# A fused conv, Mamba and MLP kernel: selective scan by quads of groups instead of pairs, depthwise sums on TensorE, and a job list by earliest end

## The chip, the cores and the metric

The kernel runs on one core of one Trainium2 chip. The metric is device time in microseconds (us) of that core, from the start to the end of one execution. All data is fp32. The engines work side by side, each through its own queue in order: PE (TensorE, matrix multiplication), DVE (VectorE), ACT (ScalarE), POOL (GpSimd) and SP, which here issues every DMA transfer.

## The reference

The input x has 8 images of 384 channels and 32 x 32 pixels. Four layers follow each other, each behind a group normalisation (32 groups of 12 channels) and with the input added to the output. Layer 0 is a Mamba block over the 1024 pixels of an image, layer 1 a patch-wise Fourier filter between two 1x1 convolutions with a depthwise 3x3 convolution and a gate, layer 2 a LayerNorm, another Mamba block and an MLP, layer 3 a depthwise 3x3 convolution. What matters here:

```python
# Mamba, layers 0 and 2: D_INNER 768, D_STATE 16, L 1024 steps, B 8 images
dt = softplus(dt @ dt_proj_w.T + dt_proj_b)
A = -exp(A_log)
def step(h, inp):
    dt_t, B_t, C_t, u_t = inp
    dA = exp(dt_t[..., None] * A)
    h = dA * h + (dt_t * u_t)[..., None] * B_t[:, None, :]
    y = einsum('bdn,bn->bd', h, C_t)
    return (h, y)
y = ys + u * D
y = y * silu(z)
out = y @ out_proj_w.T
# layer 1, in its middle; layer 3 is the same kind of convolution alone
t = conv_general_dilated(t, w_dw, padding='SAME', feature_group_count=hid)   # 3x3
g = gelu(x1) * x2
# layer 2, after its Mamba block
t = gelu(t @ mlp_w1.T + mlp_b1) @ mlp_w2.T + mlp_b2
```

## The kernel before, in words

**Chunks, pairs and quads.** The work is cut into chunks of 512 steps: 8 images x 2 halves x 2 Mamba layers = 32 chunks, 16 of layer 0 and then 16 of layer 2. A chunk has 768 channels x 16 states = 12288 recurrences, which lie 128 to a tile: 96 groups of 8 channels x 16 states, each a scan of [128, 512]. Two groups make a *pair*; 48 pairs make a chunk (PAIRS, L41). Four groups, two neighbouring pairs, make what the change calls a *quad*; there are 24 in a chunk, 768 in all.

**The steps of a pair.** `begin` (L512) issues the transfer of g, [128, 2, 512], 512 KB, from a DRAM scratch (dud) that repeats dt*u over the 16 states. `times` (L521) multiplies g by B on POOL. `decay` (L529) makes two matmuls with 32 rows each, which repeat dt over the states into two of four PSUM banks dA0 to dA3, and two exps on ACT, in place. `scan` (L540) runs two tensor_tensor_scan on DVE. On even pairs (`pool_pair`, L508, with some exceptions in EXTRA, L50) the scan writes to PSUM, in place, and DVE multiplies the result by C, from PSUM into g (L558), and copies the last column to `carry`. On the others the scan writes to g in SBUF, ACT copies the carry and POOL multiplies by C (`after_scan`, L560, the instruction at L566). `gather` (L570) sums over the states with four matmuls per two pairs into y, each into another 32 rows of PSUM; after four such sums comes the product with D, and `gate` (L588) multiplies y by silu(z) on DVE. Neighbouring pairs take turns with the two halves of the four banks, so one pair can be decayed while the other is scanned.

**The other work** is written as Python generators that are advanced between the pairs ("jobs"): `measure` (group statistics of an image), `front` (normalise, project, taps of the short convolution, dt and the spill of dt*u to DRAM), `gates` (project and silu of z), `finish` (out_proj, and in layer 2 the `mlp`), `layer1` and `layer3`. `step_dt` (L461) makes a matmul and softplus for one of six blocks of dt, then dt*u on POOL (`times_u`, tile du, L478) and four transfers to DRAM (`spill`, tile dud, L485). `mlp` (L773) streams its weights from DRAM: `load_up` (L780, tile mw1, 192 KB, four buffers) two blocks ahead of their matmuls ps_up, and `load_down` (L784, tile mw2, 384 KB, three buffers) two ahead of ps_dn. Three PSUM banks (NBANK) serve all jobs; `pipe` (L129) lets up to two units of a job fly, one stage to a call. The depthwise sums of layers 1 and 3 are eight or nine scalar_tensor_tensor on DVE per [96 or 128, 512] block (L731, L859), in PSUM.

**The order.** It is written out by hand (L906 to L945). For each pair t, in program order: begin(t+4), after_scan(t-1), times(t+2), decay(t+1), scan(t), possibly gate, then the jobs, and every second pair gather. Jobs stand in three lanes (fronts, ends, tails; L70); a lane advances its first job so that the count of pieces done follows a straight line between the job's first and last pair, from a table of expected pieces (PIECES, L66). SP's queue holds the transfers in the same program order.

Of the kernel before, what the change touches and what calls it, by code (L numbers as in the profile page):

```python
# [16 lines left out]
P = 128  # L17
# [5 lines left out]
NS = 16  # L23
# [14 lines left out]

E8 = 8
NSUB = 4  # L40
PAIRS = [(k, s, jp) for k in range(ND) for s in range(NSUB) for jp in range(2)]  # L41
NPAIR = len(PAIRS)
PER_K = NPAIR // ND
NH = ND // 2
NEAR = [(k, m) for k in range(KC) for m in range(KC) if abs(k - m) <= 1]
AHEAD = 4
NG = 8
NDT = 7
NBANK = 3
EXTRA = {"l0_": ((14,), (14,)), "l2_": ((), (6, 14))}  # L50
# [7 lines left out]
def _img(ap):  # L58
# [5 lines left out]
WAIT = "wait"  # L64

PIECES = {"gates": 8, "front0": 40, "front1": 45, "measure": 20, "end0": 5, "end1": 40,  # L66
          "layer1": 90, "layer3": 60}


class Lane:  # L70
# [3 lines left out]
    def __init__(self):  # L74
        self.jobs = deque()

    def add(self, kind, gen, first, last):
        self.jobs.append([kind, gen, first, last, 0])

    def step(self, t=None):  # L80

        for _ in range(4):
            if not self.jobs:
                return
            job = self.jobs[0]
            kind, gen, first, last, done = job
            if t is not None and done < PIECES[kind]:
                if done >= PIECES[kind] * (t + 1 - first) / (last - first):
                    return
            got = next(gen, self)  # L90
            if got is self:
                PIECES[kind] = done
                self.jobs.popleft()
            elif got is WAIT:
                return WAIT
            else:
                job[4] += 1
            if t is None:
                return
# [3 lines left out]
def tile_conv_preact_d4(ctx: ExitStack, tc: tile.TileContext, a: dict, out: bass.AP):  # L103
# [10 lines left out]
    live = {"ps": 0, "dt": 0}  # L114

    def mm(out_, lhsT, rhs, start=True, stop=True):
        nc.tensor.matmul(out_, lhsT, rhs, start=start, stop=stop)  # L117
# [11 lines left out]
    def pipe(units, deep=2):  # L129
# [4 lines left out]
        while units or flying:  # L134
# [7 lines left out]
            if units and live["ps"] < NBANK and len(flying) < deep:  # L142
# [9 lines left out]
            if units or flying:  # L152
                yield None if went else WAIT

# [27 lines left out]

    def rsqrt(out_, in_, eps):
        act(out_, in_, AF.Ln, bias=eps)
        act(out_, out_, AF.Exp, scale=-0.5)
# [13 lines left out]
    carry = const.tile([P, 2 * NPAIR], F32, name="carry")  # L199
# [9 lines left out]
    dAs = [psa.tile([P, T], F32, name=f"dA{q}") for q in range(4)]  # L209
# [3 lines left out]
    def group_stats(block):  # L213
# [3 lines left out]
        for h in range(2):  # L217
            for k in range(KC):
                v, then = block(h, k)
                nc.vector.bn_stats(st[:, k, h, :], v)  # L220
                then()
                yield
        for k in range(KC):
            nc.vector.bn_aggr(mv[:, k, :], _flat(st[:, k]))
        yield

        def group_mean(v):
# [11 lines left out]
            yield  # L239
# [6 lines left out]
        yield  # L246
# [4 lines left out]
        yield  # L251
# [4 lines left out]
        yield  # L256
        nbias = wk.tile([P, KC, 1], F32, tag="gnb", name="gnb", bufs=3)
        nc.gpsimd.tensor_mul(nbias, nmean, rstd)
        yield
# [9 lines left out]
    def load_mamba(pre):  # L269
# [4 lines left out]
        w["A"] = wk.tile([P, 2 * NPAIR], F32, tag="w_A", name="w_A", bufs=2)  # L274
# [12 lines left out]
        nc.vector.tensor_scalar_mul(w["A"], w["A"], -1.0)  # L287
# [6 lines left out]
    def load_out(w, pre):  # L294
        w["out"] = wk.tile([P, ND, C], F32, tag="w_out", name="w_out")
        load_rows(w["out"], a[pre + "out_proj"], ND)

# [6 lines left out]
    def measure(s):  # L304
# [11 lines left out]

        load(0)
# [6 lines left out]
        s["stats"] = yield from group_stats(block)  # L324
# [16 lines left out]
    def gates(s):  # L341

        z = s["z"] = [wk.tile([P, NH, T], F32, tag="z", name="z", bufs=2) for _ in range(2)]

        def evict(d):
            return lambda ps: act(z[d // NH][:, d % NH, :], ps, AF.Copy)

        yield from pipe(("ps_z", [both(project(s, d, DI), evict(d))]) for d in range(ND))
        yield
        for h in range(2):  # L350
            act(_flat(z[h]), _flat(z[h]), AF.Silu)
        s["gates"] = True
        yield

    def layer_norm(xn):
# [3 lines left out]
        yield  # L359
        for k in range(KC):  # L360
            nc.vector.tensor_sub(xn[:, k, :], xn[:, k, :], ps)
        ps_done()
        yield
# [5 lines left out]
        yield  # L369
        rsqrt(ps, ps, eps_ln)  # L370
        yield
        for k in range(KC):
            nc.vector.scalar_tensor_tensor(
                xn[:, k, :], xn[:, k, :], ln_w[:, k : k + 1], ps, ALU.mult, ALU.mult
            )
            if k == 0:
                yield
        ps_done()
        for k in range(KC):
            act(xn[:, k, :], xn[:, k, :], AF.Identity, bias=ln_b[:, k : k + 1])  # L380
        yield

    def front(s):

        c, n = s["c"], s["n"]
        xn = s["xn"] = load_half(s)
# [4 lines left out]
        yield  # L391
        yield
        for k in range(KC):
            group_norm(xn[:, k, :], xn[:, k, :], k, chunks[n - c]["stats"])
        yield
        if s["pre"] == "l2_":
            yield from layer_norm(xn)
        while n > 1 and "free" not in chunks[n - 2]:
# [14 lines left out]
        def taps(d):  # L413
            def run(ps):
                for j in (1, 2):
                    nc.vector.scalar_tensor_tensor(  # L416
# [7 lines left out]
            ("ps_in", [both(project(s, d, 0), tap(d)), taps(d)]) for d in range(ND)  # L424
# [14 lines left out]
        yield  # L439
        for h in range(2):  # L440
            act(_flat(uh[h]), _flat(uh[h]), AF.Silu)
        yield
        ps = yield from ps_tile("ps_x")
        for d in range(ND):
            mm(ps[:RX, :], w["x"][:, d, :], u[d], start=d == 0, stop=d == ND - 1)
            if d == NH - 1:
                yield
# [3 lines left out]
        yield  # L451
        bc = s["bc"] = wk.tile([P, 2, T], F32, tag="bc", name="bc", bufs=2)
        s["dt"], s["dud"] = [None] * ND, [None] * ND
# [7 lines left out]
        def step_dt(d):  # L461
# [10 lines left out]
            def plus(ps):  # L472
                v = s["dt"][d] = wk.tile([P, T], F32, tag="dt", name="dt", bufs=NDT)
                nc.vector.scalar_tensor_tensor(v, ps, 0.0, got["m"], ALU.max, ALU.add)
# [5 lines left out]
            def spill(ps):  # L480
                to = s["dud"][d] = dram.tile(
                    [2, NSUB * E8, 2, T], F32, tag="dud", name="dud", bufs=2 * ND
                )
                for j in range(4):
                    nc.sync.dma_start(  # L485
                        to[j // 2, :, j % 2, :], got["du"][32 * j : 32 * (j + 1), :]
                    )

            return [log, plus, None, times_u, spill]
# [4 lines left out]
        for d in range(ND):  # L494
            while live["dt"] >= NDT:
# [5 lines left out]
            yield  # L501
# [581 lines left out]
```

## Time and profile before

| | us |
|---|---|
| median of 3 runs | 8042.84 |
| lowest and highest | 8034.11, 8051.01 |
| the profiled execution's own time | 8035.86 |
| its span in the profile | 8034.1 |
| first scan starts | 90.5 |
| last gate of layer 0 starts | 3991.2 |
| last gate of layer 2 starts | 7884.7 |

The profiled execution was one of its own, beside the three runs. On the page, the first part gives each engine's busy time, its share of the span and the number of instructions; the second shows the span in 40 slices, with busy shares in tenths (9 is 90% or more) and under PEclk the TensorE clock that was granted. The groups give line, engine, operation, out<-in, shape and count, then busy time and mean duration (ns), then the idle time before them and what ended it. L117 and L181 are the helpers that record every matmul and every activation, so those are told apart by tile names. Each fp32 matmul is recorded as two passes. In a timeline, the columns are start, duration, engine, line, operation and count of merged instructions.

### The profile page before, as it was taken

The page shows a single profiled execution, that of the slowest core. Times are in us where ns is not written, and L with a number is a line of the kernel's source. Part 1 is how long each engine was busy: PE and PEld are TensorE (multiplying, and loading weights), DVE is VectorE, ACT ScalarE, POOL GpSimd, SP SyncE. Part 2 cuts the span into 40 slices and gives each one's busy share as a digit, 9 for nine tenths or more (in the row PEclk, how much of TensorE's full clock was granted, in tenths as well). Part 3 has the DMA queues.
Part 4 walks back from the last instruction along what each step waited for, and adds up shares of the span by engine and source line. Part 5 has one row for each costly group of instructions (what it writes and reads, how often), then busy time and mean ns, then how long its engine had stood idle before and what let it go on. Part 6 is the DMA issues. An engine that isn't in the chain of part 4 may idle for free.

```text
span 8034.1 us, 75941 instructions
## 1 busy us (share of the span) xinstructions
PE 7175.9 (89%) x23938; PEld 2930.4 (36%) x23938; DVE 5955.8 (74%) x7526; ACT 3747.6 (47%) x6393; POOL 5843.0 (73%) x2806
## 2 busy tenths in 40 slices
PE   6988898988989898998799999998999989899996
PEld 2223232322323232332343444344443444444444
DVE  4777879787887878788666686776867768677684
ACT  3445454444545444354444454444545545445542
POOL 5887877778878777777467676776767767677681
PEclk7878787887878788787798899898998989989988
DMA  5554555555455545555356565555565555655563
GB/s 136 142 140 119 132 132 125 130 131 138 126 138 129 131 122 128 136 139 136 79 142 157 137 168 153 139 161 149 158 162 146 149 152 153 167 139 160 145 173 90
DMA packets 403229, 1122.83 MB, mean 140 GB/s; under 512 B 52746, under 2 KB 106970, under 8 KB 402828
## 3 DMA queue, kind: packets, MB, share of 16 engines
q1 hardware_dynamic: 402828, 1117.98, 53.6%
q8 instruction: 192, 3.15, 0.2%
q14 instruction: 209, 1.71, 0.1%
HBM read 1042.28 MB, written 75.50 MB: 139 GB/s over the span
## 4 chain that ended last, share of the span: by engine, by line
PE 32%; DVE 8%; issue 6%; POOL 6%; ACT 3%; DMA 3%; SPq 1%; POOLq 0%; ACTq 0%; DVEq 0%
PE dA L117 7%; PE ps_dn L117 6%; POOL g L524 4%; PE y L117 4%; PE ps_up L117 4%; PE ps_z L117 3%; DVE g L545 2%; PE ps_out L117 2%; PE ps_in L117 2%; DVE dA L545 2%; POOL g L566 1%; DMA g<-dud 1%; PE ps_x L117 1%; DMA mw<-in_l_mlp_w 1%; ACT dA L181 1%
## 5 line engine op out<-in xcount | busy, mean ns | idle before, releaser
L524 POOL TENSOR_TENSOR g<-g,bc 128x1024 f32<-128x1024 f32 x1536 | 3588.7, 2353 | 14.5 <-ACT dA L181 11.3
L566 POOL TENSOR_TENSOR g<-g,bc 128x1024 f32<-128x1024 f32 x864 | 2031.6, 2351 | 1890.7 <-ACT carry L181 1109.5
L181 ACT ACTIVATE dA<-dA,w_A 128x512 f32<-128x512 f32 x3072 | 1911.5, 658 | 2708.6 <-PE dA L117 2558.4
L117 PE MATMUL dA<-dt,selr 32*128 32x512 f32 x6144 | 2224.3, 747 | 411.2 <-DVE g L558 320.0
L117 PEld LDWEIGHTS dA<-dt,selr 32*128 32x128 f32 x6144 | 641.6, 210 | 1822.9 <-DVE g L558 622.8
L545 DVE TENSOR_TENSOR_SCAN g<-dA,carry,g 128x512 f32<-128x512 f32 x912 | 1115.9, 1266 | 237.5 <-issue 116.7
L545 DVE TENSOR_TENSOR_SCAN g<-dA,g 128x512 f32<-128x512 f32 x816 | 950.5, 1206 | 456.0 <-issue 303.8
L545 DVE TENSOR_TENSOR_SCAN dA<-dA,g 128x512 f32<-128x512 f32 x720 | 840.9, 1213 | 449.8 <-issue 250.1
L117 PE MATMUL y<-g,sely 128*32 128x512 f32 x6144 | 978.7, 702 | 4.5 <-POOL g L566 4.3
L545 DVE TENSOR_TENSOR_SCAN dA<-dA,carry,g 128x512 f32<-128x512 f32 x624 | 767.2, 1274 | 208.1 <-issue 119.5
L558 DVE TENSOR_TENSOR g<-dA,bc 128x512 f32<-128x512 f32 x1344 | 878.0, 676 | 0.0
L117 PE MATMUL ps_up<-t,mw 128*128 128x256 f32 x2304 | 576.4, 402 | 67.3 <-DMA mw<-in_l_mlp_w 38.3
L117 PE MATMUL ps_z<-xf,w_in 128*128 128x512 f32 x1152 | 606.3, 667 | 0.0
L117 PE MATMUL ps_in<-xf,w_in 128*128 128x512 f32 x1152 | 584.7, 649 | 22.1 <-DVE u L416 13.8
L117 PE MATMUL ps_dn<-h,mw 128*128 128x256 f32 x2304 | 566.7, 403 | 31.7 <-ACT h L181 13.1
L117 PE MATMUL ps_out<-u,w_out 128*128 128x512 f32 x1152 | 586.9, 660 | 0.0
L117 PEld LDWEIGHTS ps_up<-t,mw 128*128 128x128 f32 x2304 | 447.5, 200 | 260.4 <-issue 93.3
L117 PEld LDWEIGHTS ps_dn<-h,mw 128*128 128x128 f32 x2304 | 453.6, 201 | 188.7 <-issue 68.0
L731 DVE SCALAR_TENSOR_TENSOR ps_dw<-tp,w1dw,ps_dw 96x512 f32<-96x512 f32 x480 | 357.5, 745 | 34.6 <-ACT ps_dw L181 25.8
L117 PEld LDWEIGHTS ps_out<-u,w_out 128*128 128x128 f32 x1152 | 236.4, 211 | 346.6 <-issue 344.6
L117 PEld LDWEIGHTS ps_z<-xf,w_in 128*128 128x128 f32 x1152 | 223.9, 208 | 377.2 <-issue 334.7
L117 PEld LDWEIGHTS ps_in<-xf,w_in 128*128 128x128 f32 x1152 | 219.3, 203 | 382.4 <-issue 292.3
(95 smaller groups left out, 5832.3 us busy)
## 6 DMA issues: line engine op xcount, KB each, us to landing
g<-dud SPq DMA_DIRECT2D x1536, 512.0 KB, 5.7
mw<-in_l_mlp_w SPq DMA_DIRECT2D x384, 192.0 KB, 4.4
mw<-in_l_mlp_w SPq DMA_DIRECT2D x192, 384.0 KB, 5.2
dud<-du SPq DMA_DIRECT2D x768, 64.0 KB, 3.1
xk<-in_x SPq DMA_DIRECT2D x48, 256.0 KB, 3.8
xf<-in_x SPq DMA_DIRECT2D x16, 768.0 KB, 7.4
x<-in_x SPq DMA_DIRECT2D x16, 768.0 KB, 8.2
x_mid<-x SPq DMA_DIRECT2D x16, 768.0 KB, 4.4
```

The lines of the kernel that those rows point to most:

```text
L117: nc.tensor.matmul(out_, lhsT, rhs, start=start, stop=stop)
L181: nc.scalar.activation(out_, in_, func, **kw)
L524: nc.gpsimd.tensor_mul(g, g, s["bc"][:, 0, :].unsqueeze(1).to_broadcast([P, 2, T]))
L545: nc.vector.tensor_tensor_scan(bank(i, j) if here else g[:, j, :], bank(i, j), g[:, j, :], 0.0 if s["c"] == 0 else carry[:, q : q + 1], AL ...
L558: nc.vector.tensor_mul(g[:, j, :], bank(i, j), s["bc"][:, 1, :])
L566: nc.gpsimd.tensor_mul(g, g, s["bc"][:, 1, :].unsqueeze(1).to_broadcast([P, 2, T]))
L731: nc.vector.scalar_tensor_tensor(_img(gate[:, j, :]) if j < 2 and t == 8 else acc, win, w1dw[:, j, t : t + 1], acc, ALU.mult, ALU.add,)
```

## The change

The kernel after works on quads.

- `begin` transfers g for four groups at once, [128, 4, 512], 1 MB, three quads ahead (AHEAD 3), in four buffers of that size instead of eight of half of it. The DRAM scratch dud is laid out accordingly.
- `decay` makes four matmuls, one on each row quadrant, into the four banks, and four exps. There is one set of banks, so the decay of quad t+1 writes the banks that quad t's scans read.
- All scans write to g in SBUF. The carry is one DVE copy of four columns. The product with C (`weigh`) is split: DVE takes groups 0 and 1, POOL groups 2 and 3 (SHARE is 2 everywhere), both from SBUF to SBUF.
- `gather` follows one quad behind, with the gate right behind the last of a block.
- The depthwise sums of layers 1 and 3 go to PE: for each of nine taps, ACT scales an identity matrix by the tap's weights, and a matmul with that diagonal and the shifted window adds into PSUM. ACT or DVE takes the sum out (in layer 3, DVE adds x to it).
- Jobs are kept in one list. Each quad gives room for so much PE and DVE work (ROOM, about 5.0 and 2.4 us of estimated work in layer 0, 6.3 and 2.4 in layer 2), and the job with the earliest end whose next piece has half its need left goes on. NEXT holds a job until the next quad; WAIT means that it cannot go on. The gates job is made per half of the channels.
- Behind each Silu or Gelu the table set of exp is loaded at once (`exp_again`).
- Buffers: the mlp's mw1 three instead of four, tpix two instead of three, t three instead of four, with acc of layer 3 apart.
- The order of a quad: scan(t), times(t+1), weigh(t), gather(t-1), begin(t+3), the jobs, decay(t+1).

```diff
-AHEAD = 4
-NG = 8
-EXTRA = {"l0_": ((14,), (14,)), "l2_": ((), (6, 14))}
+AHEAD = 3
+SHARE = {"l0_": ((2, 2, 2, 2), (2, 2, 2, 2)), "l2_": ((2, 2, 2, 2), (2, 2, 2, 2))}
...
+ROOM = {"l0_": (5.0, 2.4), "turn": (6.2, 2.4), "l2_": (6.3, 2.4)}
...
+class Jobs:
...
+    def step(self, t, room):
+        self.room = [max(min(x, y / 4), -y) + y for x, y in zip(self.room, room)]
+        for job in self.jobs:
+            job["held"] = False
+        went = True
+        while went:
+            went = False
+            for job in sorted(self.jobs, key=lambda j: j["last"]):
+                need = self.need(job)
+                if not job["held"] and job["first"] <= t and all(
+                    y == 0 or x >= y / 2 for x, y in zip(self.room, need)
+                ):
+                    went = self.piece(job)
+                    if went:
+                        break
...
+    def depthwise(pool, rows, todo):
+        taps = [(n, t) for n in range(len(todo)) for t in range(9)]
+        def diagonal(q):
+            if q < len(taps):
+                n, t = taps[q]
+                d = pool.tile([P, rows], F32, tag="diag", name="diag", bufs=4)
+                act(d[:rows], eye[:rows, :rows], AF.Copy, scale=todo[n][0][:, t : t + 1])
+                return d[:rows]
+        now = diagonal(0)
+        yield NEXT
+        for q, (n, t) in enumerate(taps):
+            if t == 0:
+                ps = yield from ps_tile("ps_dw")
+            _, window, take = todo[n]
+            then = diagonal(q + 1)
+            mm(_img(ps[:rows]), now, window(t // 3, t % 3), start=t == 0, stop=t == 8)
+            now = then
+            if t == 8:
+                take(ps[:rows])
+                ps_done()
+            if t % 3 == 2:
+                yield
...
-            return [log, plus, None, times_u, spill]
+            return [both(log, plus), None, both(times_u, spill)]
...
     def begin(s, i):
-        k, sub, jp = PAIRS[i]
-        t = s["g", i] = wk.tile([P, 2, T], F32, tag="g", name="g", bufs=NG)
+        k, sub = QUADS[i]
+        t = s["g", i] = wk.tile([P, 4, T], F32, tag="g", name="g", bufs=AHEAD + 1)
...
     def decay(s, i):
+        k, sub = QUADS[i]
+        for j in range(4):
+            rows = slice(32 * j, 32 * (j + 1))
+            mm(dAs[j], selr[rows, sub, :], s["dt"][k][rows, :])
...
+        for j in range(4):
+            act(dAs[j], dAs[j], AF.Exp, scale=s["w"]["A"][:, 4 * i + j : 4 * i + j + 1])
...
     def scan(s, i):
         g = s["g", i]
+        for j in range(4):
             nc.vector.tensor_tensor_scan(
-                bank(i, j) if here else g[:, j, :],
-                bank(i, j),
+                g[:, j, :],
+                dAs[j],
                 g[:, j, :],
...
+        if s["c"] < NCH - 1:
+            nc.vector.tensor_copy(
+                carry[:, 4 * i : 4 * i + 4].unsqueeze(2), g[:, :, T - 1 : T]
             )
...
+    def weigh(s, i):
+        own = SHARE[s["pre"]][s["c"]][i % NSUB]
+        for engine, part in ((nc.vector, slice(0, own)), (nc.gpsimd, slice(own, 4))):
+            g = s["g", i][:, part, :]
+            engine.tensor_mul(
+                g, g, s["bc"][:, 1, :].unsqueeze(1).to_broadcast([P, part.stop - part.start, T])
+            )
...
             def load_up(f):
-                w1[f] = p2.tile([P, KC, P], F32, tag="mw1", name="mw1", bufs=4)
+                w1[f] = p2.tile([P, KC, P], F32, tag="mw1", name="mw1", bufs=3)
...
+        scan(s, i)
+        if t + 1 < total:
+            times(*steps[t + 1])
+        weigh(s, i)
+        if t > 0:
+            p, q = steps[t - 1]
+            gather(p, q)
...
         if t + AHEAD < total:
-            begin(*steps[t + AHEAD])
+            p, q = steps[t + AHEAD]
+            jobs.until(lambda: p.get("dud", {}).get(QUADS[q][0]))
+            begin(p, q)
+        jobs.step(t, ROOM["turn" if n == B * NCH else s["pre"]])
         if t + 1 < total:
             decay(*steps[t + 1])
```

## The prediction

> **What bounds the kernel now.** I read the page first, then busy time by windows, the groups, the timeline of one stretch of each layer, and SP's own waits.
>
> ```profile
> PE 7175.9 (89%) x23938; PEld 2930.4 (36%) x23938; DVE 5955.8 (74%) x7526; ACT 3747.6 (47%) x6393; POOL 5843.0 (73%) x2806
> ...
> PEclk7878787887878788787798899898998989989988
> ```
>
> PE is the busiest, but at a clock of about 0.81 in the first half (Mamba layer 0 and layer 1) and 0.92 in the second (layers 2 and 3). The first scan starts at 90.5 us and the last gate at 7885; the first half ends at 3991. With 16 chunks of 24 quads (a quad is two of today's pairs) in each half, that is (3991 - 90.5) / 384 = 10.16 us a quad in the first half and (7885 - 3991) / 384 = 10.14 in the second; the ends take 90 and 150 us.
>
> ```profile
> L524 POOL TENSOR_TENSOR g<-g,bc 128x1024 f32<-128x1024 f32 x1536 | 3588.7, 2353 | 14.5 <-ACT dA L181 11.3
> L566 POOL TENSOR_TENSOR g<-g,bc 128x1024 f32<-128x1024 f32 x864 | 2031.6, 2351 | 1890.7 <-ACT carry L181 1109.5
> L117 PE MATMUL dA<-dt,selr 32*128 32x512 f32 x6144 | 2224.3, 747 | 411.2 <-DVE g L558 320.0
> L117 PE MATMUL y<-g,sely 128*32 128x512 f32 x6144 | 978.7, 702 | 4.5 <-POOL g L566 4.3
> L558 DVE TENSOR_TENSOR g<-dA,bc 128x512 f32<-128x512 f32 x1344 | 878.0, 676 | 0.0
> ```
>
> Each fp32 matmul is two passes in the trace. The next lines, from two stretches of PE's timeline, give passes at both clocks and the decay pair.
>
> ```profile
> 2202.22 5.13 PE L117 MATMUL ps_in<-xf,w_in 128*128 128x512 f32 x6
> 2210.05 2.84 PE L117 MATMUL ps_in<-xf,w_in 128*128 128x512 f32 x6
> ...
> 5499.84 2.75 PE L117 MATMUL ps_up<-t,mw 128*128 128x256 f32 x12
> 5502.53 1.07 PE L117 MATMUL y<-g,sely 128*32 128x512 f32 x8
> ...
> 5508.31 2.75 PE L117 MATMUL ps_up<-t,mw 128*128 128x256 f32 x12
> 5511.00 1.13 PE L117 MATMUL dA<-dt,selr 32*128 32x512 f32 x4
> ```
>
> Three matmuls take 2.56 us start to start at full clock (0.855 each) and double that after a gap; a decay pair on two row quadrants takes 1.06, four y matmuls on four column quadrants 1.0. Work on PE is unevenly laid: counted from the order of PE's instructions, chunks of layer 0 have quads with 10 us of projections and others with none, where PE waits for DVE and POOL.
>
> SP matters for the change: its queue is in order, and these waits stand in it.
>
> ```profile
> SPq L485 <- POOL du L478: 285.7, 92, 44.2
> ```
>
> ```profile
> 5289.70 1.95 SPq L485 DMA_DIRECT2D dud<-du  x4
> 5291.70 0.92 SPq L782 DMA_DIRECT2D mw<-in_l_mlp_w  x2
> ```
>
> ```profile
> mw<-in_l_mlp_w SPq DMA_DIRECT2D x384, 192.0 KB, 4.4
> mw<-in_l_mlp_w SPq DMA_DIRECT2D x192, 384.0 KB, 5.2
> ```
>
> Four spills (dud) take 1.9 us to issue; the mlp weights issued behind them land 4.4 or 5.2 us later. Today PE waits for them only 38 us at ps_up in all: four buffers, and pieces of the mlp lie a pair or more apart.
>
> [...]
>
> **The change, part by part**, per quad. Scans stay 4 at 1.24 us (mean of 1.21 and 1.27) = 4.96; written to SBUF or PSUM they cost alike (1206 and 1213 ns).
>
> Decay: 2 x 1.06 becomes one group of four. Bounds 0.9 (perfect) to 2.1 (no gain); I take 1.06 as for y. Weigh: DVE today has 21 to 24 of 48 pairs, 1344/768 x 0.676 = 1.18 us; after, one 1024-column multiply, 1.22[...], and POOL one 2.35 (today 1.125 x 2.35 = 2.65). With POOL's two times, 4.7, and du, 6 a chunk x 1.27 (0.32), POOL has 7.4, and 8.6 if DVE's multiply shuts it out. The wait of DVE for POOL is between 0 and 2.35, or 4.7 if two POOL operations pass. I take 0: DVE's multiply directly follows its scan, while POOL's must come over a semaphore.
>
> Depthwise: DVE loses 512 operations of 745 ns and 432 of 748 (704 us in all) and gains 48 additions (33). PE gains 1008 matmuls x 0.855 = 862 us, against 768 x 1.06 = 814 saved in decays: level. ACT gains 1008 small diagonals and some 64 more table loads of 1283 ns, loses 408 carries; from 47% it goes to some 52%, and nothing waits long for it. The carry becomes 384 copies of four columns, at some 0.15 (today's copy of one: 147 ns). PE per quad at full clock, counted from the new order: layer 0 4.72 of jobs + 2.06 = 6.8; layer 2 6.5 + 2.06 = 8.6.
>
> Order: jobs now fill every quad evenly (5.1 in most layer-0 quads of odd chunks, 5 to 8.5 in layer 2). The ring: decay starts at 0, exp and scans end at 1.1 + 0.9 + 4.96 = 7.0; the two weighs end 3.8 later (1.22, then 2.35, and waits); y (1.0) and then the jobs J stand behind that weigh, and the next-but-one decay behind the jobs. With period p, y of the earlier quad starts 10.8 - p after a decay, so p = (10.8 + 1.0 + J)/2. Layer 0: J = 4.72/0.82 = 5.8, p = 8.8; plus 0.5 for uneven quads, du behind weigh, and Silu and Gelu ahead of exps on ACT: 9.3. Layer 2: J = 6.5/0.92 = 7.1, p = 9.4.
>
> Now SP in layer 2. A step issues: g for three quads on (behind y of the last quad), then the jobs' transfers. In a step where a dt is made these are four dud, which wait for du on POOL; du stands behind two times and the weigh of the current quad. So dud goes out at scan end S + 3.8 + 1.3 = S + 5.1, the mlp weights behind it at S + 7.0, and they land at S + 11.5. The new order puts two ps_up pieces (12 matmuls) in one step, with three buffers instead of four: the second piece needs weights issued in that very step. PE then waits, its piece ends at S + 14.2, and only then the next decay: a step of 7.0 + 14.2 = 21.2 for 9.4, so 11.9 lost. I count 34 such steps; 12 steps with three ps_dn tiles and dud lose about the same (12.9); 22 with fewer tiles about 4.8; 30 steps with two ps_up pieces and no dud about 2 (weights issued at y, landing at 5 where 2.75 was needed). Sum 34 x 11.9 + 12 x 12.9 + 22 x 4.8 + 30 x 2 = 725 us[...]. The cover that hides the same transfers today (four buffers, pieces apart) is gone. The g transfers are doubled (1 MB; 5.7 to 11.4 us) but issued over a step and a half ahead of times: hidden, costing up to 2 us a quad if not.
>
> Ends: 240 + 15, the last depthwise sums on PE for those on DVE. Sum: 384 x 9.3 + 384 x 9.4 + 725 + 90 + 255 = 3571 + 3610 + 815 + 255 = 8251, against the profiled execution's own 8035.86 us (span 8034.1 and 1.8 around it): +2.7%. That execution is 7 us under the median of 8042.84, so about 8260.
>
> **Rivals.** (1) Not slower: the weights are not late, as SP may run further ahead than I think or the pieces be served from loads of the step before. Then 150 us of the 815 stay: 7590. For it speaks that DMA is half busy and waits for mw are 38 us today; against it the order of SP's queue. It decides at 815 - 220 = 595 us of stalls: below that the change gains.
> (2) [...]each of DVE's multiplies waits for one POOL operation, 2.35. DVE has 4.96 + 0.1 + 2.35 + 1.22 + 1.2 of jobs = 9.8, with POOL behind it, about 10.3: 768 x 10.3 + 600 of stalls not covered + 255 = 8765. Two operations each, 12.1: 9550 before stalls. For it: POOL is occupied 8.6 of 9.4; against it: the weigh follows DVE's own scan.
> (3) Decay quads do not run together (2.1): PE +1.0 a quad in both layers, p + 0.5: 8640.
>
> **How the numbers follow.** Forecast 8260, its own range 8040 to 8550 (p of layer 0 between 8.8 and 9.7, stalls 600 to 1000), chance 0.48; rival 1 0.27; rival 2 0.17; rival 3 0.08. Within 0.2% is about what a measurement of this kernel can tell from no change. Rival 1 gives faster 0.27, the lower edge of the forecast 0.03 more; same 0.05; slower 0.65. The range reaches from rival 1 to rival 2: 7600 to 8750.
>
> **What would show it.** dA groups of 8 passes in 1.1 us; first half near 9.3 us a quad (3570 us), second near 11.5; PE waiting some 10 us for mw at ps_up in steps where dud stands ahead; SP waiting for du at the spill line. It is wrong if ps_up waits under 300 us in all, or if DVE's multiply lasts 2 to 4 us instead of 1.2.

## The result, and the profile after

The kernel after takes 8971.74 us (median of 4 runs, 8964.76 to 8987.22), the kernel before on the same chip 8046.93 (8034.11 to 8053.04): ratio 1.1154, 95% interval 1.1134 to 1.1175. Slower, as forecast, but by 925 us where I forecast some 220; the range ended at 8750.

One number ahead of it was misread. The table of the kernel before and the prediction have the last gate of layer 0 at 3991.2 us. That gate belongs to the first chunk of layer 2; there are six gates in a chunk, and the 96th and last of layer 0 starts at 3753.3. So before, layer 0 took 9.54 us a quad and layer 2 10.76, not 10.16 and 10.14. All that follows takes the first scan, the 96th and the last gate from DVE's timeline.

| us | before | forecast | after |
|---|---|---|---|
| layer 0, 384 quads | 3662.7 (9.54) | 3571 (9.3) | 3858.7 (10.05) |
| layer 2, 384 quads | 4131.4 (10.76) | 4425 (9.4, and 815 of stalls) | 4872.9 (12.69) |
| ends | 239.9 | 255 | 253.8 |
| span of the profiled execution | 8034.1 | 8251 | 8985.4 |

The miss against the forecast is 288 us in layer 0 and 448 in layer 2. The page of the kernel after, lines that answer to those of before (busy, mean ns; behind the second bar the idle time ahead of the group):

```profile
PE 7529.0 (84%) x25954; PEld 3109.1 (35%) x25954; DVE 5744.1 (64%) x5718; ACT 4024.6 (45%) x6980; POOL 6330.4 (70%) x2710
...
L647 POOL TENSOR_TENSOR g<-g,bc 128x1024 f32<-128x1024 f32 x768 | 2504.3, 3261 | 2365.5 <-DVE g L629 1228.3
L612 POOL TENSOR_TENSOR g<-g,bc 128x1024 f32<-128x1024 f32 x1536 | 3581.5, 2351 | 14.1 <-DMA g<-dud 14.1
...
L165 PE MATMUL dA<-dt,selr 32*128 32x512 f32 x6144 | 1156.5, 673 | 53.3 <-DVE g L629 51.6
L647 DVE TENSOR_TENSOR g<-g,bc 128x1024 f32<-128x1024 f32 x768 | 1066.2, 1388 | 13.1
L165 PE MATMUL ps_up<-t,mw 128*128 128x256 f32 x2304 | 677.1, 456 | 450.6 <-DMA mw<-in_l_mlp_w 448.4
L165 PE MATMUL ps_dn<-h,mw 128*128 128x256 f32 x2304 | 613.5, 428 | 257.7 <-DMA mw<-in_l_mlp_w 225.1
L165 PE MATMUL ps_dw<-tp,diag 96*96 96x512 f32 x1152 | 644.2, 698 | 148.6 <-ACT diag L232 147.4
```

Three things are new. PE waits for the mlp's weights (mw), 448 us at ps_up where it was 38. POOL's product with C (L647) lasts 3261 ns where the same operation as `times` (L612) lasts 2351. And PE waits for ACT's diagonals at ps_dw. Every engine is busy for a smaller share of the span than before.

**Weights behind spills.** SP's waits, and then SP's and PE's timeline over one step of layer 2:

```profile
SPq L579 <- POOL du L572: 1593.0, 188, 43.9
```

```profile
6561.08 0.52 SPq L602 DMA_DIRECT2D g<-dud  x1
6573.91 1.73 SPq L579 DMA_DIRECT2D dud<-du  x4
6575.69 5.86 SPq L862 DMA_DIRECT2D mw<-in_l_mlp_w  x4
```

```profile
6562.00 2.86 PE L165 MATMUL ps_up<-t,mw 128*128 128x256 f32 x12
6578.29 4.79 PE L165 MATMUL ps_up<-t,mw 128*128 128x256 f32 x12 [13.44 <-DMA mw<-in_l_mlp_w]
6583.02 1.14 PE L165 MATMUL dA<-dt,selr 32*128 32x512 f32 x8
```

SP stands at the spill (dud) from 6561.6 to 6573.9 us, waiting for POOL's du; only then does it issue the weights, and the second ps_up piece of the step waits 13.44 us for them. The next decay (dA) stands behind it in PE's queue. The piece then takes 4.79 us where the one ahead took 2.86: its first passes start 0.43 us apart instead of 0.22, and the granted clock is 0.50 from 6578.2 to 6581.0 us where it was 1.00 from 6562.0 to 6565.0: the half clock. This is the step that the prediction describes. SP waited 286 us at this spill before, 1593 after.

**DVE beside POOL.** DVE and POOL in layer 0, in order of time:

```profile
2202.93 4.64 POOL L612 TENSOR_TENSOR g<-g,bc 128x1024 f32<-128x1024 f32 x2
...
2205.28 2.33 DVE L638 COPY carry<-g 128x4 f32<-128x4 f32 x1
2207.64 1.23 DVE L647 TENSOR_TENSOR g<-g,bc 128x1024 f32<-128x1024 f32 x1
2207.75 3.32 POOL L647 TENSOR_TENSOR g<-g,bc 128x1024 f32<-128x1024 f32 x1 [0.17 <-DVE carry L638]
...
2216.18 0.17 DVE L638 COPY carry<-g 128x4 f32<-128x4 f32 x1
```

The copy of four columns takes 0.17 us at 2216.18, where POOL is idle, and 2.33 where POOL is in its `times`: it ends as these end, at 2207.6. Then DVE's product starts 0.11 us ahead of POOL's, and POOL's lasts 3.32 instead of 2.35. Over the whole run the copy takes 645 ns in the mean for a median of 170, and POOL's product 3261 ns in the mean for the 2351 of `times`. So in these operations DVE and POOL hold each other up; by what mechanism the trace doesn't show.

**Diagonals behind ACT's queue.** PE and ACT in layer 0:

```profile
2405.36 1.10 PE L165 MATMUL ps_dw<-tp,diag 96*96 96x512 f32 x2
...
2406.10 1.29 ACT L232 ACTIVATE spm<-spm 128x512 f32<-128x512 f32 x2
2407.30 1.15 ACT L232 ACTIVATE diag<-eye,w1dw 96x96 f32<-96x96 f32 x4
...
2407.71 7.92 PE L165 MATMUL ps_dw<-tp,diag 96*96 96x512 f32 x10 [1.25 <-ACT diag L232]
```

Only one diagonal is made ahead. The second one stands behind softplus steps (spm) in ACT's queue, and PE, with all that follows in its own, waits for it.

### The profile page after: what moved, and what is told of

Same layout as the page of the kernel before. It is cut to its first block, busy times and chain, and to the rows that moved or that the text cites. A ratio compares the mean times of both kernels' runs of the same rounds, so it can differ in the third digit from the quotient of the medians.

```text
span 8985.4 us, 76368 instructions
## 1 busy us (share of the span) xinstructions
PE 7529.0 (84%) x25954; PEld 3109.1 (35%) x25954; DVE 5744.1 (64%) x5718; ACT 4024.6 (45%) x6980; POOL 6330.4 (70%) x2710
## 5 line engine op out<-in xcount | busy, mean ns | idle before, releaser
L647 POOL TENSOR_TENSOR g<-g,bc 128x1024 f32<-128x1024 f32 x768 | 2504.3, 3261 | 2365.5 <-DVE g L629 1228.3
L612 POOL TENSOR_TENSOR g<-g,bc 128x1024 f32<-128x1024 f32 x1536 | 3581.5, 2351 | 14.1 <-DMA g<-dud 14.1
L629 DVE TENSOR_TENSOR_SCAN g<-dA,carry,g 128x512 f32<-128x512 f32 x1536 | 1845.4, 1263 | 1437.4 <-issue 884.3
L629 DVE TENSOR_TENSOR_SCAN g<-dA,g 128x512 f32<-128x512 f32 x1536 | 1751.0, 1202 | 1140.2 <-issue 606.6
L165 PE MATMUL y<-g,sely 128*32 128x512 f32 x6144 | 1322.2, 656 | 313.1 <-POOL g L647 192.0
L165 PE MATMUL dA<-dt,selr 32*128 32x512 f32 x6144 | 1156.5, 673 | 53.3 <-DVE g L629 51.6
L647 DVE TENSOR_TENSOR g<-g,bc 128x1024 f32<-128x1024 f32 x768 | 1066.2, 1388 | 13.1
L165 PE MATMUL ps_dw<-tp,diag 96*96 96x512 f32 x1152 | 644.2, 698 | 148.6 <-ACT diag L232 147.4
L165 PEld LDWEIGHTS dA<-dt,selr 32*128 32x128 f32 x6144 | 337.0, 192 | 664.9 <-DVE g L629 273.1
L165 PE MATMUL ps_dw<-xp,diag 128*128 128x512 f32 x864 | 442.6, 651 | 96.8 <-ACT diag L232 95.8
L165 PEld LDWEIGHTS ps_dw<-tp,diag 96*96 96x96 f32 x1152 | 198.0, 186 | 574.6 <-ACT diag L232 313.5
```

Source lines behind the costliest of these rows:

```text
L612: nc.gpsimd.tensor_mul(g, g, s["bc"][:, 0, :].unsqueeze(1).to_broadcast([P, 2, T]))
L629: nc.vector.tensor_tensor_scan(g[:, j, :], dAs[j], g[:, j, :], 0.0 if s["c"] == 0 else carry[:, 4 * i + j : 4 * i + j + 1], ALU.mult, ALU.add,
L647: engine.tensor_mul(g, g, s["bc"][:, 1, :].unsqueeze(1).to_broadcast([P, part.stop - part.start, T]))
```

## The experiments

The lines suggest three costs: S (weights behind spills on SP), P (DVE's copy and product and POOL's multiplies hold each other up), D (diagonals late on ACT). Theory: S is what was forecast, and P and D are what it left out. Rivals: S is an effect of slow quads; or the diagonals cost PE time as such. Differences below are against 8971.7. The runs were made on several chips and at several times, on which the kernel before took 8047 to 8056 us, so a difference of some 20 us tells nothing. The layers are those of the profiled execution.

| run | us, median of 4 | ratio to before, 95% interval | layer 0 | layer 2 |
|---|---|---|---|---|
| 1 spill one quad later | 8589.7 | 1.0650 to 1.0696 | 3847 | 4480 |
| 2 diagonals three ahead | 8786.4 | 1.0896 to 1.0930 | 3726 | 4790 |
| 3 DVE's product and copies from PSUM | 8725.9 | 1.0825 to 1.0857 | 3705 | 4765 |
| 4 all three | 8147.5 | 1.0102 to 1.0136 | 3557 | 4335 |
| 5 and g's transfer last | 7817.5 | 0.9698 to 0.9727 | 3553 | 4025 |
| 6 sums on DVE | 8780.7 | 1.0887 to 1.0919 | 3728 | 4805 |
| 7 five, sums on DVE | 8151.4 | 1.0093 to 1.0148 | 3605 | 4290 |
| 8 seven, POOL's groups first | 8120.9 | 1.0066 to 1.0100 | 3608 | 4286 |
| 9 after, weights loaded once | 8189.7 | 1.0157 to 1.0188 | 3852 | 4081 |
| 10 five, weights loaded once | 7691.6 | 0.9538 to 0.9566 | 3551 | 3886 |
| 11 carry on ACT | 9193.3 | 1.1398 to 1.1437 | 3927 | 5013 |
| 12 both edits on SP's order | 8291.0 | 1.0285 to 1.0316 | 3856 | 4192 |
| 13 carry on POOL | 9014.8 | 1.1165 to 1.1202 | 3888 | 4874 |
| 14 product from PSUM | 8786.7 | 1.0891 to 1.0924 | 3737 | 4806 |
| 15 ten, half of ps_dn | 7664.6 | 0.9500 to 0.9529 | 3554 | 3872 |

**Run 1, S: the spill a stage later.** du and its four transfers are issued in different calls, one quad apart.

```diff
-            return [both(log, plus), None, both(times_u, spill)]
+            return [both(log, plus), None, times_u, spill]
```

> The four dud transfers of a block go out one quad after its dt*u, so SP no longer waits for POOL ahead of the MLP weights. Theory S (weights held behind the spill stretch layer 2): PE's waits for mw at ps_up and ps_dn fall from 448 and 225 us to under 200 together, SP's wait for du from 1593 to under 300, the time to about 8350 us, all of it in the second half. Theory D (diagonals held on ACT) and theory P[...]: the waits for mw fall but y, the exps or the three buffers end next, and the time stays above 8750.

It gained 382 us, nearly all in layer 2 (393 in the profiled execution, and 12 in layer 0), but ends at 8590 where theory S had some 8350. PE's waits for weights in this run:

```profile
PE ps_up L165 <- DMA mw<-in_l_mlp_w: 272.1, 64, 5.8
PE ps_dn L165 <- DMA mw<-in_l_mlp_w: 66.9, 28, 7.5
```

The longest is 5.8 us at ps_up where it was 13.4. SP waits 58 us for du where it was 1593, but 272 us remain at ps_up: the weights still stand behind the g transfer, which waits for y.

**Run 2, D: diagonals three taps ahead**, in the same four buffers.

```diff
-        now = diagonal(0)
+        made = [diagonal(q) for q in range(3)]
...
-            then = diagonal(q + 1)
-            mm(_img(ps[:rows]), now, window(t // 3, t % 3), start=t == 0, stop=t == 8)
-            now = then
+            made.append(diagonal(q + 3))
+            mm(_img(ps[:rows]), made[q], window(t // 3, t % 3), start=t == 0, stop=t == 8)
```

> Diagonals are made three taps ahead instead of one, in the same four buffers, so the next quad's first three lie on ACT ahead of the exps. Theory D: PE's wait for diag falls from 243 us to under 80 and the time to about 8650. Theory S: the first half gains at most 100 us and the second nothing, about 8880. Theory P: no change beyond 0.5%.

It gained 185 us where theory D had some 320; 133 of them are in layer 0. PE's own waits for diagonals went from 243 to 83 us. The matmuls stayed as they were, so what it gained was the wait.

**Run 3, P: groups 0 and 1 in place in PSUM**, DVE multiplies from there and copies two carries from there; POOL copies the two others. No DVE operation of a quad then reads two SBUF tensors.

```diff
-                g[:, j, :],
+                dAs[j] if j < 2 else g[:, j, :],
...
-            nc.vector.tensor_copy(
-                carry[:, 4 * i : 4 * i + 4].unsqueeze(2), g[:, :, T - 1 : T]
-            )
+            for j in range(2):
+                nc.vector.tensor_copy(carry[:, 4 * i + j : 4 * i + j + 1], dAs[j][:, T - 1 : T])
...
+        for j in range(2):
+            nc.vector.tensor_mul(g[:, j, :], dAs[j], s["bc"][:, 1, :])
+        g = g[:, 2:4, :]
+        if s["c"] < NCH - 1:
+            nc.gpsimd.tensor_copy(
+                carry[:, 4 * i + 2 : 4 * i + 4].unsqueeze(2), g[:, :, T - 1 : T]
+            )
+        nc.gpsimd.tensor_mul(g, g, s["bc"][:, 1, :].unsqueeze(1).to_broadcast([P, 2, T]))
```

> No DVE operation beside POOL has two SBUF tensor inputs or copies from SBUF to SBUF: groups 0 and 1 are scanned in place in PSUM and multiplied from there by two DVE instructions of 512 columns, their carries copied from PSUM; POOL copies the other two carries. Theory P: POOL's product falls from 3261 to 2350 ns, the carry from 645 ns for four columns to under 200 a copy, y's second half no longer waits, and the first half falls by about 400 us, the whole to about 8450. Theories S and D: the operations get shorter as told but PE waits on weights and diagonals all the same, and the time stays above 8800.

It gained 246 us, 154 in layer 0; theory P had some 520. The groups on its page:

```profile
L651 POOL TENSOR_TENSOR g<-g,bc 128x1024 f32<-128x1024 f32 x768 | 1808.0, 2354 | 1502.8 <-DVE g L629 1445.2
L645 DVE TENSOR_TENSOR g<-dA,bc 128x512 f32<-128x512 f32 x1536 | 976.2, 678 | 0.0
```

POOL's product is back at 2354 ns, and DVE's two halves (2 x 678) cost 1356, no more than the 1388 of the one that waited. PE's waits show both what it brought and what it costs, first of the kernel after, then of run 3:

```profile
PE y L165 <- POOL g L647: 192.0, 240, 3.3
PE y L165 <- DVE g L647: 90.1, 94, 3.3
```

```profile
PE dA L165 <- DVE g L645: 442.9, 180, 14.6
```

PE's waits at y for the two products, 282 us, are nearly gone (26 us). But the banks are now held until DVE has multiplied out of them, and the next decay waits 443 us for that, where it waited 52 us for scans.

**Run 4, all three edits.**

> The three edits together. If S, D and P each hold a part that does not cover the others, the gains add up: about 7750 us, under the kernel before. If they hide each other, it is not better than the best single one by more than 200 us. If the single set of PSUM banks (decay behind scan behind decay) is the limit, it stays above 8200.

8147.5: 824 us less, where the three alone make 382 + 185 + 246 = 813. They add; the 7750 of the expectation would have needed the larger gains that were expected of each. Layer 0 is at 9.26 us a quad.

**Run 5, and the g transfer behind the jobs' transfers** on SP, so that the weights don't wait for y.

```diff
-        if t + AHEAD < total:
-            p, q = steps[t + AHEAD]
-            jobs.until(lambda: p.get("dud", {}).get(QUADS[q][0]))
-            begin(p, q)
         jobs.step(t, ROOM["turn" if n == B * NCH else s["pre"]])
+        if t + AHEAD < total:
+            p, q = steps[t + AHEAD]
+            jobs.until(lambda: p.get("dud", {}).get(QUADS[q][0]))
+            begin(p, q)
```

> The three edits of e4_three, and begin moved behind the jobs of its quad, so that SP sees a quad's MLP weights ahead of the 1 MB transfer of g and ahead of its wait for y. Theory S: PE's wait at ps_up for mw falls from 277 us to under 100, layer 2 from some 273 us a chunk to 262, the time to about 7980. Rival (the three buffers alone hold the weights back, whatever stands ahead of them): the wait stays above 200 us and the time above 8100.

7817.5, 330 less again, and 2.9% faster than the kernel before (0.9698 to 0.9727): a version that beats both. PE's wait at ps_up for weights is 102 us.

**Run 6, the depthwise sums back on DVE**, alone: the loop over taps with diagonals is replaced by nine operations on DVE or ACT in PSUM, in the manner of before.

```diff
-            mm(_img(ps[:rows]), now, window(t // 3, t % 3), start=t == 0, stop=t == 8)
...
+                if t == 0:
+                    act(acc, win, AF.Copy, scale=w)
+                else:
+                    vector.scalar_tensor_tensor(acc, win, w, acc, ALU.mult, ALU.add)
```

> The changed kernel with the depthwise sums of layers 1 and 3 back on DVE, nine operations a block in PSUM; nothing else undone. Theory D and the plain count: PE loses 1087 us of ps_dw and some 240 us of waits for diag, DVE gains about 700 and has room; about 8600 us. Rival (PE's time is hidden behind the ring of decay, scan and weigh): within 100 us of 8970; rival (DVE[...] becomes the bound): slower than 8970.

8780.7: it gains 191, about as much as making the diagonals earlier (185), and fits none of the three expectations. So moving the sums to PE, as the change does it, lost 191 us.

**Runs 7 and 8, the same on top of the edits for S and P**, in 8 with groups 2 and 3 decayed and scanned first.

> e5_loads_first with the depthwise sums on DVE. If the moved sums cost apart from the rest, 250 to 350 us under e5_loads_first, about 7700, and under the kernel before. If the ring of one bank set is what is left, no gain over e5_loads_first.

> e7_all_dw_dve with groups 2 and 3 decayed and scanned first, so that POOL's product starts while DVE scans groups 0 and 1. If y's wait for POOL's product still holds the ring, 0.5 to 1 us a quad: 400 us under e7_all_dw_dve. If PE and SP set the pace by now, the same within 1%.

8151.4 and 8120.9, both some 300 us over run 5, and no expectation for 7 had a loss. PE's longest wait in it:

```profile
PE dA L165 <- DVE g L636: 1177.7, 403, 12.6
```

In run 5 this wait of the decay for DVE's product out of the PSUM banks is 497.6 us. So once the diagonals are in time, the sums on PE gain 334 us here. Why isn't settled. With the sums in its queue, DVE gives the banks back later; but in run 8, where groups 0 and 1 come last, the same wait is 329.8 us. And the granted clock differs: 0.86 in run 7 and 0.83 in run 8, 0.93 in run 5, so PE may also be slower at the work that it keeps. No run here separates the two. Turning the groups' order moved the time by 31 us, some 0.4%, and the intervals of the two runs overlap.

**Runs 9 and 12, S whole.** In 9 two blocks of each weight are loaded once and used in place of all others, so what is left out is the loading of the others and the use of their numbers; in 12 the two edits on SP's order are made alone.

```diff
-                w1[f] = p2.tile([P, KC, P], F32, tag="mw1", name="mw1", bufs=3)
-                nc.sync.dma_start(w1[f], a["l2_mlp_w1"][f])
+                if ("up", f % 2) not in kept:
+                    t = kept["up", f % 2] = p2.tile([P, KC, P], F32, tag="mw1", name="mw1", bufs=3)
+                    nc.sync.dma_start(t, a["l2_mlp_w1"][f])
+                w1[f] = kept["up", f % 2]
...
```

> Leaves out the reloading of the mlp's weights: two blocks of each are loaded once and used for all, so that no ps_up or ps_dn ever waits for a transfer and SP issues none of these. Theory (layer 2's loss is lateness of these weights, forecast at 815 us): 8972 goes down by 700 to 820, to about 8200, all of it in layer 2 (4873 us to about 4100), layer 0 unchanged at 3859. Rival (the waits for weights only stand where PE would wait for DVE and POOL anyway, and the two edits on SP's order gained by something else): down by less than 450, above 8520.

> The kernel after with both edits on SP's order alone (the spill of dt*u one quad later, and the g transfer issued behind the jobs' transfers), diagonals and port as they are. If the costs add: 8972 - 382 - 330 = 8260, layer 0 near 3850 and layer 2 near 4150. Rival: the 330 of the second edit could only be had once DVE, POOL and ACT were relieved; then this run is above 8450.

9 gained 782 us, 792 in layer 2 and 7 in layer 0; 12 gained 681 (expected 712). The theory stands: the loads, as the kernel after makes them, cost 782 us, and since run 12 moves the same bytes, order on SP alone takes back seven eighths of it.

**Runs 11, 13 and 14, which half of P.** 11: ACT copies the carry. 13: POOL does, right ahead of its product. 14: the product is made from PSUM as in run 3, but DVE copies groups 2 and 3's carry from SBUF.

```diff
-            nc.vector.tensor_copy(
-                carry[:, 4 * i : 4 * i + 4].unsqueeze(2), g[:, :, T - 1 : T]
-            )
+            act(carry[:, 4 * i : 4 * i + 4].unsqueeze(2), g[:, :, T - 1 : T], AF.Copy)
```

```diff
+            nc.gpsimd.tensor_copy(
+                carry[:, 4 * i : 4 * i + 4].unsqueeze(2), s["g", i][:, :, T - 1 : T]
+            )
```

> The kernel after with the carry copied by ACT instead of DVE, still from SBUF; the products with C as they are. It splits what the third experiment gained (246 us). If the carry on DVE was the cost (384 copies at 645 ns where I took 150): down by 120 to 190, to about 8810. If it is the shutting out between DVE's and POOL's products (POOL 3261 ns where I took 2351): down by less than 60, since the next wait, of DVE's product for POOL's times, takes the copy's place.

> The kernel after with the carry copied by POOL, right ahead of its product with C, and the products as they are: DVE has no copy that can wait for POOL, and its product follows the scan directly. The wait on the copy sums to (0.645 - 0.17) x 384 = 182 us in after, that on DVE's product to (1.388 - 1.224) x 768 = 126. If freeing the copy is what counts: down by 100 to 180, near 8830. If the product takes over the wait, because POOL is still in its times when the last scan ends: within 50 us of 8972, and DVE's product then lasts some 1.6 to 1.7 us in the mean.

> The other half of the third experiment: groups 0 and 1 are scanned in place in PSUM and DVE multiplies them from there, but the carry of groups 2 and 3 stays a DVE copy from SBUF to SBUF (128 x 2). If the shutting out between the two products was the cost (POOL 3261 ns for 2351): down by some 200 of the 246 us, near 8770. If the copy was: near 8900, with the copy still at some 0.6 us.

11 was 222 us slower, which neither expectation of it had. ACT's timeline in it:

```profile
2204.60 0.21 ACT L232 ACTIVATE carry<-g 128x4 f32<-128x4 f32 x1 [3.01 <-issue]
```

The copy takes 0.21 us, but ACT's queue stands 3 us at it until the last scan ends, with softplus and the next quad's work behind it. Before, ACT copied carries too, but with the next pair's decay already ahead of them in its queue. 13 was 43 us slower, 24 by its ratio to the kernel before beside it, which is no clear difference: the copy on DVE as such cost nothing that can be had back by moving it to POOL. 14 gained 185 of the 246. The groups of 13, then of 14:

```profile
L646 POOL TENSOR_TENSOR g<-g,bc 128x1024 f32<-128x1024 f32 x768 | 2523.5, 3286 | 1296.1 <-DVE g L629 1243.7
L646 DVE TENSOR_TENSOR g<-g,bc 128x1024 f32<-128x1024 f32 x768 | 1015.3, 1322 | 356.4 <-POOL carry L640 356.4
```

```profile
L638 DVE COPY carry<-g 128x2 f32<-128x2 f32 x384 | 93.1, 242 | 13.2
...
L650 POOL TENSOR_TENSOR g<-g,bc 128x1024 f32<-128x1024 f32 x768 | 1806.9, 2353 | 2851.1 <-DVE g L629 1487.4
```

With the product from PSUM, the copy from SBUF falls to 242 ns by itself, presumably because POOL, 0.9 us earlier with its product (2353 ns for 3261), is mostly through with `times` when the scans end. In 13 DVE's product lasts 1322 ns, not the 1600 or more that was expected: the wait stands ahead of it, 356 us for POOL's copy, and replaces the waits that were removed. The product is the larger part of P; the copy's long waits were mostly its consequence.

**Runs 10 and 15, what is left of layer 2.** 10 is run 5 with the weights loaded once; 15 leaves out every second matmul of ps_dn as well.

```diff
-                        for f in range(NFH):
+                        for f in range(0, NFH, 2):
```

> As the run before, but from the kernel with all four edits (7817.5), and again with the reloading of the mlp's weights left out. It asks what holds layer 2 at 10.5 us a quad there against my 9.4. If it is what remains of the waits for weights (100 us at ps_up) and of their half clock: about 7680. If PE is full in layer 2 (3386 busy of 3700 us): within 40 us of 7817.

> The tenth run's kernel, which leaves out the reloading of the mlp's weights, and here every second matmul of ps_dn too: 576 of 1152 (1152 of 2304 passes; ps_dn is busy 548.9 us there, so 274 us of PE's work are gone in layer 2). If PE is full in layer 2 (3097 busy of 3300 us): down by 200 to 274 from 7691.6. If DVE, POOL and the ring through them set the pace there: down by less than 100.

10 gained 126 (expected 137): what remained of S in run 5. Layer 2 is then at 10.12 us a quad, not 9.4. 15 gained 27 us, for 274 us less work on PE, and only 15 of them in layer 2, so the thought that PE's work alone is the bound falls. Busy time over the same stretch of layer 2, of 10 and then of 15 (columns: window, length, busy us of PE, PEld, DVE, ACT, POOL, PE clock, DMA share, GB/s):

```profile
4100.00:7400.00 3300.00, 3096.54 (x12473) 1538.63 (x12473) 2297.20 (x2927) 1814.88 (x3005) 2419.95 (x1315) 0.96 0.52 124
```

```profile
4100.00:7400.00 3300.00, 2984.97 (x11530) 1385.91 (x11527) 2296.66 (x2929) 1828.09 (x3016) 2416.33 (x1315) 0.93 0.52 124
```

PE has less to do and a lower granted clock, 0.93 for 0.96 (the kernel before had 0.86 beside each of the two). By my estimate that gives part of it back: 3% of some 9.2 us busy a quad is some 0.3, or 110 us over the layer. In the same window PE's wait for DVE's product before a decay doubles:

```profile
PE dA L165 <- DVE g L644: 105.0, 48, 8.8
```

```profile
PE dA L165 <- DVE g L644: 221.1, 95, 8.9
```

So a second limit seems close behind PE: the one set of banks, which DVE must empty before the next decay. How the remainder is shared among clock, banks and uneven quads isn't settled.

The same stretch of layer 2 (4100 to 7400 us) counted by quads, from one decay on PE's timeline to the next:

| us a quad | under 8 | 8 to 10 | 10 to 12 | 12 to 15 | 15 to 20 | over 20 |
|---|---|---|---|---|---|---|
| after, 260 quads | 37 | 62 | 47 | 45 | 34 | 35 |
| run 9, 309 | 45 | 102 | 81 | 52 | 27 | 2 |
| run 10, 324 | 56 | 117 | 88 | 50 | 13 | 0 |
| run 15, 324 | 62 | 102 | 92 | 57 | 11 | 0 |

## Why the prediction was right, and where it failed

**Right: the weights behind the spill.** I priced 725 us of stalls, and 90 of half clock, which were an estimate of mine that no run here shows on its own; run 9 takes 782 us away with the weights. PE's own waits for weights in the kernel after are 448 + 225 = 673 us. The single steps are as forecast: 21.2 us was worked out for a step with two ps_up pieces behind a spill, 34 times, and 22.3 for 12 with ps_dn. Of 260 quads counted 35 last over 20 us, 22.5 in the mean, which makes 52 of 384 if the rest of the layer is alike; without the reloads (run 9) 2 of 309 are left. Rival 1, that weights are not late, is out. So is rival 3: the eight passes of four decays take 1.14 us at full clock (at 6583.02, granted clock 1.00; I took 1.06, rival 3 2.1), 1.51 in the mean of all quads.

The prediction has PE at half clock "after a gap", and its example is the 5.13 us at 2202.22. The gap ahead of that is short: in the 17 us before 2199.04, PE is idle once, for 1.74 us. The granted clock is 0.51 from 2182.0 to 2186.5 us, 1.00 from 2186.5 to 2197.3 and 0.53 from 2202.2 to 2207.2. How long a gap must be isn't shown here.

```profile
2199.04 3.25 PE L117 MATMUL dA<-dt,selr 32*128 32x512 f32 x4 [1.74 <-DVE g L545]
```

**Failed: "The wait of DVE for POOL is between 0 and 2.35 ... I take 0."** The reason given, that DVE's multiply follows its own scan, holds only between the two products: DVE's starts first in all 768 quads, by 0.11 us in 316 of them, and POOL's is the one that lasts longer, 3261 ns for 2351. That much the ring's 3.8 us has in it ("1.22, then 2.35, and waits"). But POOL can still be in its `times` when the scans end, and DVE's copy and product wait for it: (645 - 170) x 384 + (1388 - 1224) x 768 = 182 + 126 = 308 us, with 1224 ns as the product's median, which is the 1.22 of the forecast. The copy's price, "at some 0.15", came from a copy of one column out of PSUM and is no price for one within SBUF beside POOL, 645 ns in the mean. With its consequences P was worth 246 us (run 3), 185 of it by moving the product alone (run 14). Rival 2 is the right wait at the wrong size: not 2.35 for each multiply, but 308 / 768 = 0.40 a quad for copy and product together.

**Failed: ACT "goes to some 52%, and nothing waits long for it".** A share of busy time doesn't tell when an instruction is reached in an in-order queue. One diagonal ahead is less than softplus and exps take (a tap's two passes 1.10 us at 2405.36; two softplus steps 1.29 at 2406.10, four exps of 661 ns in the mean), and PE's whole queue stood behind the matmul: 185 us (run 2), 133 of them in layer 0. (ACT's share itself fell, to 45% of a longer span.)

**The ring, term by term.** These are means over the quads of a layer, the last two left out, from the timelines of PE, DVE and POOL; each column starts where the one before it ends.

| us | decay to end of scans | to end of POOL's product | to end of y | to the next-but-one decay | half the sum |
|---|---|---|---|---|---|
| layer 0, forecast | 7.0 | 3.8 | 1.0 | 5.8 | 8.8, and 0.5 added |
| layer 0, after | 7.99 | 4.15 | 2.14 | 5.83 | 10.06 |
| layer 0, run 4 | 7.52 | 2.83 | 2.02 | 6.16 | 9.27 |
| layer 2, forecast | 7.0 | 3.8 | 1.0 | 7.1 | 9.4, and the stalls |
| layer 2, run 9 | 7.63 | 3.88 | 2.29 | 7.48 | 10.64 |
| layer 2, run 10 | 7.48 | 2.66 | 2.56 | 7.57 | 10.14 |

**Layer 0.** The two terms that were too small are y, which ends 2.14 us behind POOL's product and not 1.0, and the way from the decay to the end of the scans, though the scans alone take 4.68 us for my 4.96. POOL's product ends only 0.35 later than forecast. D and P alone, 133 + 154 = 287 us, make the miss of 288, and run 4 with both mended has 9.26 us a quad for the forecast's 9.3. That agreement is partly luck: in run 4 POOL's product ends 1.0 earlier than the ring had it, which offsets half of what scans, y and jobs take more.

**Failed: "Layer 2: J = 6.5/0.92 = 7.1, p = 9.4."** With no late weights it is 10.63 (run 9), with D and P mended too 10.12 (run 10). Again y is the term: "y (1.0)" took 2.56 us in run 10. Its first matmul starts 1.3 us after POOL's product has ended, right behind the decay ahead of it in PE's queue: PE comes to it late, and the ring has no term for that. Uneven quads would explain it. Run 10 has 13 of 324 quads over 15 us and 50 between 12 and 15, and none under 7, so short quads can't make up for long ones; layer 0 got 0.5 for that and layer 2 nothing. But no run evened them out, so this cause is argued and not shown. The terms of layer 2's miss of 448 us are: stalls -23 (792 in this layer for 815); D, P and the order of the g transfer 194 (4080.6 - 3886.3, run 9 to run 10); and 276 that remain in run 10 (0.72 x 384).

**The reading of before.** With 9.54 and 10.76 instead of 10.16 and 10.14, the forecast's 9.3 and 9.4 would have read as a gain of 2 to 3% in one layer and 13% in the other, the heavier one; that would have been a reason to doubt 9.4. The sum against the span wasn't touched by it, since the forecast was built from the kernel after.

**The range** joined the costs as rivals, one or another, when they add: the forecast's stalls with P and D are 8260 + 246 + 185 = 8691 before the missing term of layer 2.

## What to carry to other kernels

In an in-order DMA queue, a transfer that waits for late work (a spill, a buffer behind a reduction) belongs behind those that wait for nothing: here two edits of order took back 681 us (1.1154 to 1.0300 of the time before). When operands move from PSUM to SBUF, go again through each operation that DVE and POOL can have under way side by side, the small copies too (here a copy took 2.33 us for 0.17, and POOL's product 3261 ns for 2351), and ask what holds a PSUM bank longer when an operand goes back there (in run 3 the decay waits 443 us for DVE where it waited 52). Price a diagonal or any helper by its place in its queue, not by the engine's busy share (the late diagonals cost 185 us with ACT 45% busy). A period worked out from mean work came out too low here, 9.4 us for 10.1; count the distribution of the quads beside the mean.

## What the runs showed of the hardware that I had not expected

- A DVE copy of 128x4 within SBUF takes 0.17 us beside an idle POOL and 2.33 behind POOL's `times` (mean over all 645 ns); the 128x1 copies out of PSUM take 141 and 149 ns in the mean (768 each, runs 3 and 14).
- When DVE's 1.23 us product starts 0.11 us ahead of POOL's, POOL's goes from 2.35 to 3.32 us.
- DVE's product as two halves with one operand in PSUM (2 x 678 ns) costs no more than the whole within SBUF beside POOL's (1388 ns with its waits).
- With less work on PE its granted clock in layer 2 was lower, 0.93 for 0.96 (runs 15 and 10).
- PE went to half clock behind one idle stretch of 1.74 us (kernel before, at 2199 us: granted clock 1.00 from 2186.5 to 2197.3 us, 0.53 from 2202.2 to 2207.2).
